# Which blocks issue their row transfers at once in a fused attention and mixture-of-experts kernel

## The chip, the core and the metric

The kernel runs on one core of one Trainium2 chip. TensorE (PE in the profile) multiplies matrices, VectorE (DVE) and ScalarE (ACT) do elementwise work, GpSimd (POOL) issues the indirect transfers, and SyncE (SP) issues the plain ones. Each engine works through its own list of instructions in a fixed order and waits on semaphores where another engine or a transfer has to be done first. The metric is device microseconds from start to end of the program, as a median over runs.

## The reference

The input x has 4 images of 256 channels and 64 x 64 pixels, in float32. Layer 0 adds an attention over each pixel's 3 x 3 neighbours. Layer 1 adds a windowed average over 64 tokens, and then a mixture of 8 experts of which each token uses its best two. Only that last part bears on the change:

```python
logits = tokens.astype(jnp.float32) @ router_w.astype(jnp.float32).T
probs = jax.nn.softmax(logits, axis=-1)
rw, re = jax.lax.top_k(probs, TOP_K)
...
for e in range(E):
    h = jax.nn.gelu(tokens @ w1[e] + b1[e], approximate=False)
    y = h @ w2[e] + b2[e]
    out = out + combine[:, e:e + 1] * y
```

## The kernel before

The 16384 tokens are cut into 32 blocks of 512 (`NB` is 32). For each block the main loop interleaves four generators: `produce` (normalise, project), `attend` (neighbour attention), `tail` (windowed average, router, store of the block's own part of the output, L685) and `ranks`, two blocks behind `attend`, which works out the row of each token in a table by experts.

**The row transfers.** `rows_in` is a table in HBM with a region for each expert. A token goes there twice, once for each of its two experts. `give(t, c)` in `ranks` (L782) is one indirect transfer of 128 token rows from SBUF to `rows_in`; a block has eight of them (4 values of t, 2 of c). They are issued by POOL (L783 in the profile). This text calls them row transfers.

**Groups and slots.** Blocks are grouped: 13 groups of two and then 6 groups of one (`GROUPS`, L85). An expert's work comes in slots of 256 rows, and there are 135 slots, numbered 0 to 134. Group 0 has 1 slot, groups 1 to 12 have 8 each, groups 13 to 17 (blocks 26 to 30) have 4 each, and the last group (block 31) has 18. So slots 101, 105, 109, 113 and 117 are the first of blocks 27 to 31.

**What a slot does** (`experts`, L889): `fetch` (L906) reads its 256 rows from `rows_in` into a tile `sx`, by SP (L912). It waits for all row transfers of the groups up to its own. `pixels` transposes them on PE (L936), `hidden` is the first product and the gelu (L948, L954), `output` the second product (L967), with bias and weight on DVE (L971, L972). `add` (L977) then adds the 256 result rows to the output in HBM by two indirect transfers that accumulate, issued by POOL (L985). This text calls them the adds, a and b of a slot. Both wait until the adds of the slot before have landed (`behind`), since two slots can hold the same token. The order of a slot's steps on PE is L936 of slot m+2, half of L967 of slot m, L948 of slot m+1, the other half of L967. The tile `sx` has 9 buffers (`rowp`, L113), so `fetch` of slot m waits for the adds of slot m-9.

**Who issues the row transfers when.** Blocks below `first_of[2]`, which is 4, issue them on the spot, in `ranks`. Those are passed through `paced` (L509), which makes them wait for the latest gelu (L954) or copy of the attention weights (L565) on ACT. Blocks from 4 on put theirs into the list `waiting`. `give_rows(2)` (L883) takes two from that list behind each slot's two adds, and `in_turn` (L871) keeps the order of adds and row transfers on POOL. `fetch` calls `give_rows(0, k)`, which issues all that is left of the groups up to its own.

Of the kernel before, what the change touches and what calls it, by code (L numbers as in the profile page):

```python
# [62 lines left out]
def hybrid_block_kernel(ctx: ExitStack, tc: tile.TileContext, ins: dict, out: bass.AP):  # L63
# [8 lines left out]
    NB = B * NBI  # L72
# [14 lines left out]
    first_of = [sum(GROUPS[:k]) for k in range(len(GROUPS))]  # L87
# [421 lines left out]
    def paced(inst):  # L509


        if latest:
            tc.add_manual_dep(
                inst.ins, latest[-1].name,
                mybir.DependencyInfo(mybir.DependencyClass.Sync, mybir.DependencyReason.DATA),
                reason="pace of the indirect transfers",
            )
        return inst
# [218 lines left out]
    def ranks(g):  # L737
        if not 0 <= g < NB:
            return
        k, j = where[g]  # L740
# [30 lines left out]
        def dispatch(inst):  # L771

            for i in range(k + 1):
                tc.declare_no_dep(
                    inst, group=f"dispatch_{i}", reason="no two tokens have one row"
                )
            tc.declare_no_dep(inst, group="fetch", reason="fetched rows are not written again")
            tc.add_to_no_dep_group(f"dispatch_{k}", inst)
            dispatched[k].append(inst)
            return inst  # L780

        def give(t, c):  # L782
            return nc.gpsimd.indirect_dma_start(  # L783
                out=rows_in[:, :],
                out_offset=bass.IndirectOffsetOnAxis(ap=rows[:, c, t : t + 1], axis=0),
                in_=tok[:, t, :], in_offset=None,
            )


        for t in range(NT):  # L790
            for c in range(2):
                if g < first_of[2]:
                    dispatch(paced(give(t, c)).ins)
                else:
                    waiting.append((k, lambda t=t, c=c: in_turn(
                        dispatch(give(t, c).ins), adds[-1:], given_rows
                    )))
            yield
# [72 lines left out]
    def in_turn(inst, others, own):  # L871

        for d in others:
            tc.add_manual_dep(
                inst, d.name,
                mybir.DependencyInfo(
                    mybir.DependencyClass.NoSync, mybir.DependencyReason.SCHED_ONLY
                ),
                reason="order of the indirect transfers",
            )  # L880
        own.append(inst)

    def give_rows(n, k=None):  # L883

        while waiting and (n > 0 or k is not None and waiting[0][0] <= k):
            waiting.pop(0)[1]()
            n -= 1
# [162 lines left out]
    for g in range(NB + 2):  # L1050
        load_xs(g + AHEAD + 2)
        channel_stats(g + AHEAD)
        gens = [attend(g), ranks(g - 2), tail(g - 1), produce(g + 1)]
        if g == 1:
            load_experts()
        n = 0
        while gens:
            for gen in list(gens):
                if next(gen, gens) is gens:
                    gens.remove(gen)  # L1060
                    continue
                n += 1
                follow(g + min(n / STEPS.get(g, 26), 0.999))
# [51 lines left out]
```

## Time and profile before

| | us |
|---|---|
| median of 3 runs (lowest to highest) | 1396.13 (1393.88 to 1398.09) |
| the profiled execution | 1398.9 |
| its span, first to last instruction | 1397.2 |
| PE busy | 1262.4 (90%) |
| DVE busy | 988.1 (71%) |
| ACT busy | 803.6 (58%) |
| POOL busy | 743.0 (53%) |

The profile is of one execution. Its span is 1.7 us shorter than that execution's time, and that time is 2.8 us above the median of the runs. The mean granted TensorE clock is 0.964 of full speed. An engine's busy time is an average over stages; which engine or transfer sets the pace has to be read stage by stage. In a row of a timeline, the numbers are start and duration in us, and the bracket gives the engine's idle time before the instruction and what is taken to have ended it. In a row of windows, busy times stand in the order PE, PE weight load, DVE, ACT, POOL, each with its count of instructions, then the granted clock, the busy share of the DMA engines and GB/s.

### The profile page before, as it was taken

The numbers are of one execution on the slowest core, as the hardware profiler recorded it, in microseconds if no ns is written. First come the engines' busy times: TensorE is split into PE (matmuls) and PEld (weight loads), VectorE is DVE, ScalarE is ACT, GpSimd is POOL, SyncE is SP. The second block draws the span as 40 slices with busy tenths as digits, with TensorE's granted clock in tenths as the row PEclk, the third lists the DMA queues.
The fourth block names the chain that finished last, engine by engine and source line by source line (L and its number), as shares of the span: only waits on it lengthen the run. The fifth ranks groups of instructions, "written<-read, shape, count | busy, mean of one in ns | idle before, by whom it ended". The sixth has DMA issues, their size and how long they took to land. (4 is left out here: it accounts for less than half of the span.)

```text
span 1397.2 us, 23159 instructions
## 1 busy us (share of the span) xinstructions
PE 1262.4 (90%) x6224; PEld 1049.8 (75%) x6224; DVE 988.1 (71%) x4649; ACT 803.6 (58%) x1605; POOL 743.0 (53%) x615
## 2 busy tenths in 40 slices
PE   5898999899999999999999999999999999859740
PEld 4677777688888878888888888888878887648530
DVE  4499988587887877787878778787867788613220
ACT  1434457666666665777776666666767665324310
POOL 2023414555665655655666556565655666654444
PEclk8999999899999999999999999999999999989975
DMA  9624444566656565666665563656565446665543
GB/s 326 245 91 131 138 160 111 148 147 142 165 111 174 125 151 128 156 151 158 155 143 129 125 159 79 159 120 147 108 168 119 90 92 151 152 143 82 81 54 38
DMA packets 147792, 190.42 MB, mean 136 GB/s; under 512 B 13776, under 2 KB 121936, under 8 KB 147536
## 3 DMA queue, kind: packets, MB, share of 16 engines
q0 software_dynamic: 51168, 71.07, 29.0%
q1 hardware_dynamic: 94000, 116.42, 26.9%
q10 hardware_dynamic: 2496, 1.45, 0.4%
q8 instruction: 52, 0.85, 0.3%
q14 instruction: 76, 0.62, 0.2%
HBM read 98.31 MB, written 90.59 MB: 135 GB/s over the span
## 5 line engine op out<-in xcount | busy, mean ns | idle before, releaser
L985 POOL DMA_INDIRECT out<-sx x270 | 431.1, 1597 | 443.8 <-DVE sx L972 126.8
L783 POOL DMA_INDIRECT rows_in<-tok,rows x256 | 267.3, 1044 | 124.2 <-issue 67.3
L967 PE MATMUL psy<-w,h 128*128 x1080 | 285.5, 387 | 10.0 <-DVE sx L971 7.2
L948 PE MATMUL psh<-xc,w1s 128*128 128x256 f32 x1080 | 260.5, 383 | 3.8 <-issue 2.8
L967 PEld LDWEIGHTS psy<-w,h 128*128 128x128 f32 x1080 | 201.7, 192 | 59.5 <-DVE sx L971 30.3
L971 DVE TENSOR_TENSOR sx<-psy,b2b 128x256 f32<-128x256 f32 x270 | 113.2, 419 | 158.2 <-PE psy L967 127.5
L948 PEld LDWEIGHTS psh<-xc,w1s 128*128 128x128 f32 x1080 | 200.9, 192 | 30.3 <-issue 4.0
L954 ACT ACTIVATE h<-psh,w1s 128x256 f32<-128x256 f32 x270 | 116.9, 478 | 104.9 <-PE psh L948 101.6
L940 ACT COPY xc<-ptx 128x512 f32<-128x512 f32 x135 | 79.6, 590 | 151.7 <-PE ptx L936 106.8
L455 PE MATMUL psv<-vo,x 128*128 128x257 f32 x528 | 131.8, 394 | 16.4 <-DVE x L437 8.7
L455 PEld LDWEIGHTS psv<-vo,x 128*128 128x128 f32 x528 | 100.9, 197 | 33.3 <-issue 7.4
L481 PE MATMUL psq<-x,qk 128*128 128x512 f32 x256 | 123.6, 592 | 0.0
L535 PE MATMUL pss<-x,q 128*128 128x256 f32 x512 | 123.2, 384 | 0.1
L572 PE MATMUL psc<-v,pT 128*128 128x256 f32 x512 | 121.8, 380 | 0.1
L572 PEld LDWEIGHTS psc<-v,pT 128*128 128x128 f32 x512 | 97.3, 190 | 26.9 <-issue 11.5
L936 PE MATMUL ptx<-ident,sx 128*128 128x128 f32 x540 | 84.2, 279 | 36.8 <-DMA sx<-rows_in 36.2
L936 PEld LDWEIGHTS ptx<-ident,sx 128*128 128x128 f32 x540 | 67.1, 146 | 57.3 <-issue 39.0
L535 PEld LDWEIGHTS pss<-x,q 128*128 128x128 f32 x512 | 95.8, 192 | 13.6 <-ACT xc L603 0.9
L972 DVE TENSOR_SCALAR sx<-sx 128x256 f32<-128x256 f32 x270 | 99.0, 367 | 4.3 <-issue 0.2
L954 ACT ACT_TABLE_LOAD x78 | 100.1, 1283 | 1.3
L552 ACT ACTIVATE pe<-logits,stop 128x259 f32<-128x259 f32 x128 | 64.3, 503 | 53.8 <-DVE stop L548 53.4
L576 DVE SCALAR_TENSOR_TENSOR xT<-psc,den,xT 128x256 f32<-128x256 f32 x128 | 55.7, 476 | 55.9 <-PE psc L572 49.3
(187 smaller groups left out, 2195.6 us busy)
## 6 DMA issues: line engine op xcount, KB each, us to landing
sx<-rows_in SPq DMA_DIRECT2D x135, 272.0 KB
xs<-in_x SPq DMA_DIRECT2D x32, 512.0 KB
xT<-in_xT SPq DMA_DIRECT2D x32, 512.0 KB
out<-xT SPq DMA_DIRECT2D x32, 512.0 KB
x<-in_x SPq DMA_DIRECT2D x24, 640.0 KB
x<-in_x SPq DMA_DIRECT2D x8, 576.0 KB
out<-sx POOLq DMA_INDIRECT x270
rows_in<-tok,rows POOLq DMA_INDIRECT x256
```

What stands on the lines that cost most here:

```text
L455: nc.tensor.matmul(ps, t[:, ci, j * P : (j + 1) * P], vo[:, ci, :], start=(ci == 0), stop=(ci == NC - 1),)
L481: nc.tensor.matmul(ps, qk[:, ci, co * P : (co + 1) * P], t[:, ci, W : W + TB], start=(ci == 0), stop=(ci == NC - 1),)
L535: nc.tensor.matmul(ps, q[:, ci, t * P : (t + 1) * P], t_[:, ci, t * P : t * P + NK], start=(ci == 0), stop=(ci == NC - 1),)
L572: nc.tensor.matmul(ps[:, u, :], pT[:, u, j, :], vals[j], start=(j == 0), stop=(j == 1))
L783: return nc.gpsimd.indirect_dma_start(out=rows_in[:, :], out_offset=bass.IndirectOffsetOnAxis(ap=rows[:, c, t : t + 1], axis=0), in_=tok[: ...
L936: nc.tensor.transpose(pt[:, c, t * P : (t + 1) * P], xs[:, t, c * P : (c + 1) * P], ident)
L948: nc.tensor.matmul(ps[:, f, :], w1s[:, o : o + P], xc[:, ci, :], start=(ci == 0), stop=(ci == NC - 1),)
L954: inst = nc.scalar.activation(h[:, f, :], ps[:, f, :], AF.Gelu, bias=w1s[:, F1 + f : F1 + f + 1])
L967: nc.tensor.matmul(ps[:, t, :], h[:, f, t * P : (t + 1) * P], w2[:, e, f, :], start=(f == 0), stop=(f == NC - 1),)
L971: nc.vector.tensor_add(ys[:, t, :], ps[:, t, :], b2b[:, e, :])
L972: nc.vector.tensor_scalar_mul(ys[:, t, :], ys[:, t, :], xs[:, t, bass.ds(e + C, 1)])
L985: inst = nc.gpsimd.indirect_dma_start(out=out, out_offset=bass.IndirectOffsetOnAxis(ap=xs[:, t, C + E : C + E + 1].bitcast(U32), axis=0), ...
```

## The change

Blocks 4 and 5, and blocks 30 and 31, now issue their row transfers in `ranks` as blocks 0 to 3 do. Before them, `give_rows(0, k)` empties the list of everything that belongs to their own group or an earlier one. Blocks 6 to 29 stay as they were.

```diff
         for t in range(NT):
             for c in range(2):
-                if g < first_of[2]:
+                if not first_of[3] <= g < NB - 2:
+                    give_rows(0, k)
                     dispatch(paced(give(t, c)).ins)
                 else:
                     waiting.append((k, lambda t=t, c=c: in_turn(
```

`first_of[3]` is 6 and `NB - 2` is 30. Lines behind this place are two higher in the new file: L985 becomes L987, L912 becomes L914.

## The prediction

> **What bounds the kernel now.** I read the table of busy times first, then windows by stage, then POOL's timeline of the last 220 us, and beside it the timelines of PE and DVE for the same slots, the chain of waits last. The windows show two regimes.
>
> ```profile
> 300.00:340.00 40.00, 39.97 (x207) 33.73 (x206) 34.04 (x164) 29.34 (x57) 25.80 (x22) 1.00 0.58 136
> ...
> 1080.00:1120.00 40.00, 40.00 (x203) 34.02 (x202) 31.62 (x161) 27.00 (x55) 25.43 (x19) 1.00 0.51 101
> ...
> 1160.00:1200.00 40.00, 38.28 (x198) 32.26 (x197) 34.20 (x184) 19.75 (x38) 27.89 (x22) 1.00 0.54 113
> 1200.00:1240.00 40.00, 26.21 (x120) 21.31 (x118) 15.15 (x65) 14.07 (x29) 27.80 (x23) 0.93 0.70 171
> 1240.00:1280.00 40.00, 33.06 (x150) 27.45 (x151) 11.27 (x29) 14.20 (x29) 19.15 (x13) 0.86 0.57 105
> ```
>
> Up to about 1170 us PE is full and sets the pace. After that it has holes, and the two largest are waits for a fetch behind the row transfers of blocks 30 and 31:
>
> ```profile
> 1214.44 1.09 PE L936 MATMUL ptx<-ident,sx 128*128 128x128 f32 x4 [5.21 <-DMA sx<-rows_in]
> ...
> 1246.38 1.08 PE L936 MATMUL ptx<-ident,sx 128*128 128x128 f32 x4 [13.82 <-DMA sx<-rows_in]
> ```
>
> They look like 19 us to be had. POOL says otherwise. Counting pairs of adds back from the last (1386.67, slot 134), 1181.72 is slot 104 and 1249.06 slot 113:
>
> ```profile
> 1181.72 1.60 POOL L985 DMA_INDIRECT out<-sx  x1 [2.29 <-DVE pj L626]
> 1183.62 1.58 POOL L985 DMA_INDIRECT out<-sx  x1 [0.30 <-DVE step L837]
> 1185.51 1.00 POOL L783 DMA_INDIRECT rows_in<-tok,rows  x1 [0.30 <-DVE first_row L860]
> 1186.81 0.98 POOL L783 DMA_INDIRECT rows_in<-tok,rows  x1 [0.30 <-issue]
> 1190.29 1.60 POOL L985 DMA_INDIRECT out<-sx  x1 [2.51 <-DVE tst_f L498]
> ...
> 1242.84 1.59 POOL L985 DMA_INDIRECT out<-sx  x1 [0.30 <-issue]
> 1249.06 1.57 POOL L985 DMA_INDIRECT out<-sx  x1 [4.64 <-issue]
> ...
> 1282.06 1.54 POOL L985 DMA_INDIRECT out<-sx  x1 [3.08 <-DMA out<-sx]
> 1283.90 1.54 POOL L985 DMA_INDIRECT out<-sx  x1 [0.30 <-issue]
> 1288.38 1.54 POOL L985 DMA_INDIRECT out<-sx  x1 [2.93 <-DVE sx L972]
> ```
>
> And two rows of DVE's timeline:
>
> ```profile
> 1228.82 0.35 DVE L972 TENSOR_SCALAR sx<-sx 128x256 f32<-128x256 f32 x1
> ...
> 1230.47 0.35 DVE L972 TENSOR_SCALAR sx<-sx 128x256 f32<-128x256 f32 x1
> ```
>
> They are slot 113's result, counted back the same way: ready at 1230.82, added at 1249.06. It was not the result that the add waited for, nor was it for any slot from 103 on; the engine that a bracket names had long been done. What it waits for is the landing of the slot before. The chain of waits has that as one piece:
>
> ```profile
> 1277.44 3.78 DMA out<-sx
> ```
>
> So a slot of the add chain takes 1.54 + 0.30 (add a), then 4.6 from issue of add b to issue of the next a, 6.45 in all. From slot 113 to the last, 21 intervals take 137.61, or 6.55 each. The last L972 ends at 1347.09 and the last add starts at 1388.51. From slot 103 (1173.37) the end is the start of the add chain plus its links. The PE holes lie under it.
>
> **The change part by part.** The instructions of PE, DVE and ACT stand in the same order in both built programs. POOL's list changes in two places, and three SP transfers move.
>
> *Blocks 4 and 5, on POOL.* Block 4's eight row transfers now stand ahead of slot 0's adds. Their rows are ready at 191.97 (L768). The pace waits are for the copy L565 that ends at 192.35, a gelu at 198.20 and a copy at 199.25. At 0.98 + 0.30 each the eight end near 205.9, and POOL is idle before from 179.6 to 207.21, so they cost 0; without that gap they would be 10.2. The four row transfers of block 5 between slot 2's adds a and b wait for a copy at 234.2, so add b moves from 235.20 to about 237.1, and four more follow. Queued behind are add 3 and the small L339 that `tail` needs: about 0.6 later than at 244.56. Its reader L620 runs at 254.21, so that is 0 too; 9 us of slack would have to go first. The first slot of blocks 4 and 5 can be fetched 17 us earlier, but PE takes it up only at 285.88, with the data landed near 267: no gain. On SP a load L130 and a store L685 move behind the fetch that needs slot 3's landing, near 252 against 251.05 and 265.97. PE is full after 280: 0.
>
> *Blocks 30 and 31, on POOL.* Before, their 16 transfers go two by two into the wait for a landing. That wait is 3.1 us, two of them take 2.6, so they are nearly free: 6.49, 6.51 and 6.55 for slots 105, 106 and 107. After, the built order is four behind slot 104's adds, four between a and b of slot 106, four behind slot 108, two behind 109, two behind 110. Their pace waits are for the gelus of slots 106 to 112, the last of which ends at 1219.86 even before, ahead of the transfer that waits for it, so they hold nothing up. Nine slots, 104 to 112, then take:
>
> - four behind a pair: 1.60 + 0.30 + 1.57 + 0.30 + 4 x 1.28 = 8.89, twice: 17.8
> - four between the adds: 1.60 + 0.30 + 5.12 + 4.6 = 11.6
> - two behind a pair: 6.5, twice: 13.0
> - none (105, 107, 111, 112): 6.45 each, 25.8
>
> Sum 68.2. Measured before, 1181.72 to 1249.06: 67.3. But that holds 8.7 of late landings (9 x 6.45 = 58.05, and 0.07 for each of eight slots with two transfers): slots 104, 108, 109, 110 and 112 take 8.57, 8.99, 8.07, 7.48 and 8.13, each while a burst is on the queues (fetches at 1181.11, 1211.04 and 1242.80, the eight blank rows from 1216.72). These bursts move, they don't go. The first now falls under a gap that POOL fills itself; block 30's fetches go off at about 1205.7 instead of 1211, onto slot 106; a store L685 on SP moves behind two more fetches and with the blank rows lies mostly under slot 108; block 31's fetches go off near 1240. No row shows this mixture. None exposed gives +0.9 in all, all of it exposed +9.6; I take 4.0 (1.7 as slot 112 for the last burst, 1.8 on slots 106 and 107, 0.5 on 109), by those rows. So the adds of slot 113 start 4.9 later.
>
> *What it buys.* Block 30 is in 5 us earlier, block 31 only about 2, since its last transfer still goes at 1237 against 1239.45. PE loses most of the 5.21 and 2 of the 13.82. Both lie under the chain: 0. If the cover were gone, it would be 7.
>
> Sum: +4.9 on the profiled execution's 1398.9, 1403.8; on the median of 1396.13, which is 2.8 lower, 1401.0.
>
> **A rule against the trace.** POOL's row is 1044 ns for a row transfer, and in the tail 0.98 with 0.30 of gap. The Trainium skill ("DMA: Bandwidth & Descriptors", section "Anatomy of one DMA — SWDGE (gpsimd) path") lists about 50 ns of dispatch and calls descriptor generation small: "You can emit a lot of descriptors before the incremental cost shows up". By that a batch of four is nearly free, every slot keeps 6.45, and nine take 58.05 + 4.0 = 62.1, 5.2 less than before: 1390.9. By the trace they take 72.2. I go by the trace, which has 526 such instructions of 1.0 to 1.6 us.
>
> **The rivals.**
>
> *The bursts stay hidden (+0.9 to +2.5, about 1398).* For: two of the gaps become POOL's own. Against: slot 106's landing is open.
>
> *The early batch was the cause of a stall (on the other side of the line).* Between 253 and 266 PE makes almost no headway: DVE idles 8.2 until 266.04, and PE is busy 4.25 of the 10 us from 260. Granted clock is 1.00 until 261, so the clock follows the stall. POOL runs from 248.91 to 265.16 without a pause, ten row transfers and two adds, and the change dissolves exactly that batch. If the batch is the cause, 8 us return where PE is the bound and carry through to slot 103: 1396.13 - 8 + 4.9 = 1393.0. It decides if the recovered time exceeds the tail's slip. Against: the eights at 94.92, 117.12, 143.50 and 166.95 did PE no such harm, and nothing names a link.
>
> *PE's tail holes count after all.* If add 113 came when its data came, 7 us would return: 1389. Slot 113's 18 us of slack speaks against.
>
> *Nothing moves in effect*: 1396.
>
> **How the numbers follow.** Likeliest: tail slip, 0.55, with 3 to 8: 1399 to 1404. Hidden bursts 0.20; stall gone 0.17; PE holes 0.04; nothing 0.04. About 0.3%, 4.2 us, is what a measurement can tell from no change: 1391.9 to 1400.3. Slower: three quarters of the first case, 0.42. Faster: half of the stall case, the PE holes, and 0.06 for the spread of runs (2 us to either side): 0.18. The same: 0.40. The range 1391 to 1405 leaves out part of the faster cases and slips above 9.
>
> **What would show it.** Right: on POOL, slot 106's adds about 7 apart and slots 104 and 108 near 8.9; adds of slot 113 3 to 8 later against the adds of slot 104, the links after it still 6.45, PE's 5 us hole gone without effect. Wrong: row transfers that take well under 1 us in a batch; a shorter 104 to 113; a PE that is busy from 253 to 266 and a slot 103 that starts some 8 earlier; or adds that start within 0.4 of their slot's L972.

## The result, and the profile after

The changed kernel takes 1390.8 us (median of ten runs, 1387.14 to 1393.86) against 1395.63 for the kernel before (ten runs, 1392.59 to 1399.9): ratio 0.9961, 95% interval 0.9943 to 0.9978, or 0.4% faster. The forecast was 1401.0, in a range from 1391 to 1405, most likely slower. The profiled execution of the changed kernel has a span of 1390.9 at a granted clock of 0.973; before it was 1397.2 at 0.964. Lines behind L790 stand two further down in the changed kernel: the adds are L987, `ptx` is L938.

What was not expected stands early. Windows of the kernel before (columns: window and length, then busy time and instructions of PE, PEld, DVE, ACT and POOL, granted clock, DMA share, GB/s):

```profile
240.00:260.00 20.00, 18.82 (x106) 16.60 (x105) 14.87 (x85) 11.24 (x22) 13.46 (x13) 1.00 0.50 140
260.00:280.00 20.00, 14.25 (x52) 10.79 (x52) 8.38 (x36) 11.63 (x22) 8.13 (x7) 0.74 0.68 158
```

and the same windows after, with two of the tail:

```profile
240.00:260.00 20.00, 20.00 (x113) 17.91 (x112) 17.53 (x101) 12.14 (x26) 11.39 (x10) 1.00 0.73 195
260.00:280.00 20.00, 20.00 (x92) 16.01 (x91) 13.04 (x44) 13.71 (x26) 10.08 (x8) 1.00 0.53 110
...
1200.00:1240.00 40.00, 23.51 (x101) 19.22 (x101) 8.23 (x21) 10.39 (x22) 25.20 (x19) 0.79 0.75 172
1240.00:1280.00 40.00, 35.49 (x172) 29.54 (x173) 13.77 (x35) 16.22 (x33) 18.63 (x12) 1.00 0.52 83
```

PE is busy 40 of 40 us between 240 and 280, where it was busy 33.07. The waits of the kernel before from 250 to 272 us show what stood there (engine and line, what it waited for, us in total, times, longest):

```profile
DVE so_far L759 <- remote: 8.2, 1, 8.2
ACT v L459 <- remote: 5.8, 2, 3.3
PEld psv L455 <- remote: 5.1, 1, 5.1
```

"remote" is a wait whose release the profile can put down to no instruction. DVE and ACT wait for results of PE (`psk`, `psv`) whose matmuls have long ended by PE's own rows; the third row is PE's own next weight load, held behind them. After the change there is no such row. The time is won there and kept: the last copy L681 ahead of that stretch comes 0.8 us later than before (256.1 against 255.3), the first of the next block 9.4 earlier (290.4 against 299.8), and add a of slot 104 comes 10.9 earlier (1170.84 against 1181.72).

The tail went as forecast, with a loss. POOL's timeline after (start, length, what; in the bracket the idle time before it and its releaser):

```profile
1170.84 1.61 POOL L987 DMA_INDIRECT out<-sx  x1 [2.31 <-DVE pj L626]
1172.75 1.59 POOL L987 DMA_INDIRECT out<-sx  x1 [0.30 <-DVE step L839]
1174.65 1.09 POOL L783 DMA_INDIRECT rows_in<-tok,rows  x1 [0.30 <-DMA sx<-rows_in]
...
1179.87 1.61 POOL L987 DMA_INDIRECT out<-sx  x1 [0.30 <-DVE tst_f L498]
...
1186.47 1.57 POOL L987 DMA_INDIRECT out<-sx  x1 [3.11 <-DVE nt_f L353]
1188.35 0.99 POOL L783 DMA_INDIRECT rows_in<-tok,rows  x1 [0.30 <-issue]
...
1193.45 1.61 POOL L987 DMA_INDIRECT out<-sx  x1 [0.30 <-issue]
1198.20 1.56 POOL L987 DMA_INDIRECT out<-sx  x1 [3.14 <-DVE first_row L862]
...
1204.72 1.55 POOL L987 DMA_INDIRECT out<-sx  x1 [3.09 <-DVE sx L974]
...
1213.54 1.61 POOL L987 DMA_INDIRECT out<-sx  x1 [0.30 <-issue]
...
1241.53 1.56 POOL L987 DMA_INDIRECT out<-sx  x1 [3.01 <-DVE sx L973]
```

Slot 104, with four row transfers behind its pair, takes 1170.84 to 1179.87, or 9.03; slot 106, with four between a and b, 11.73; slot 108 8.82. From slot 104 to slot 113 it is 70.69 instead of 67.34: 3.35 lost. Of PE's two holes the first is gone and the second is longer, since, counted from slot 104, PE comes to it some 5 us earlier and the data only 3:

```profile
1232.35 1.09 PE L938 MATMUL ptx<-ident,sx 128*128 128x128 f32 x4 [16.17 <-DMA sx<-rows_in]
```

So the two profiles read as follows: about 11 us won at 256 to 290 us, 3 to 5 lost in the tail. Whether the change wins the eleven, or the profile of before had met an accident, only runs can tell.

### The profile page after: what moved, and what is told of

Same layout as the page of the kernel before. It is cut to its first block, busy times and chain, and to the rows that moved or that the text cites. A ratio compares the mean times of both kernels' runs of the same rounds, so it can differ in the third digit from the quotient of the medians.

```text
span 1390.9 us, 23174 instructions
## 1 busy us (share of the span) xinstructions
PE 1259.6 (91%) x6224; PEld 1049.5 (75%) x6224; DVE 988.8 (71%) x4649; ACT 803.3 (58%) x1605; POOL 739.3 (53%) x615
## 5 line engine op out<-in xcount | busy, mean ns | idle before, releaser
L987 POOL DMA_INDIRECT out<-sx x270 | 430.8, 1596 | 419.7 <-DVE sx L974 88.1
L783 POOL DMA_INDIRECT rows_in<-tok,rows x256 | 264.0, 1031 | 144.6 <-issue 65.8
L455 PE MATMUL psv<-vo,x 128*128 128x257 f32 x528 | 129.7, 389 | 12.3 <-DVE x L437 8.7
L938 PE MATMUL ptx<-ident,sx 128*128 128x128 f32 x540 | 84.1, 278 | 43.7 <-DMA sx<-rows_in 43.7
L455 PEld LDWEIGHTS psv<-vo,x 128*128 128x128 f32 x528 | 99.9, 195 | 27.9 <-issue 7.4
L938 PEld LDWEIGHTS ptx<-ident,sx 128*128 128x128 f32 x540 | 66.8, 146 | 64.8 <-issue 47.6
```

Of the source, the lines that this page charges most:

```text
L455: nc.tensor.matmul(ps, t[:, ci, j * P : (j + 1) * P], vo[:, ci, :], start=(ci == 0), stop=(ci == NC - 1),)
L783: return nc.gpsimd.indirect_dma_start(out=rows_in[:, :], out_offset=bass.IndirectOffsetOnAxis(ap=rows[:, c, t : t + 1], axis=0), in_=tok[: ...
L938: nc.tensor.transpose(pt[:, c, t * P : (t + 1) * P], xs[:, t, c * P : (c + 1) * P], ident)
L987: inst = nc.gpsimd.indirect_dma_start(out=out, out_offset=bass.IndirectOffsetOnAxis(ap=xs[:, t, C + E : C + E + 1].bitcast(U32), axis=0), ...
```

## The experiments

The kernels were run in six series. In each, all kernels ran one after another on one chip, and the kernel before was timed beside them; the quoted expectations call a series a call. All ratios are to the kernel before of the same series, with 95% intervals. One table first, since the kernel before turned out to have two levels:

| series | before, us | stall in it | changed | early half alone | late half alone | four behind slots 0 to 3 |
|---|---|---|---|---|---|---|
| first comparison | 1395.63 | profiled: yes | 0.9961 | | | |
| A | 1379.92 | profiled: no | | 1.0002 (0.9990 to 1.0015) | 1.0040 (1.0024 to 1.0055) | 0.9990 (0.9979 to 1.0001) |
| B | 1396.14 | profiled: yes | 0.9964 (0.9951 to 0.9977) | | | |
| C | 1381.08 | not profiled | 1.0036 (1.0020 to 1.0052) | 1.0003 (0.9993 to 1.0012) | | 1.0003 (0.9990 to 1.0015) |
| D | 1381.65 | not profiled | | 1.0000 (0.9987 to 1.0014) | | 0.9998 (0.9986 to 1.0010) |
| E | 1396.31 | not profiled | 0.9952 (0.9936 to 0.9969) | 0.9930 (0.9905 to 0.9956) | | 0.9925 (0.9901 to 0.9950) |
| F | 1395.49 | not profiled; a variant of it: yes | 0.9955 (0.9940 to 0.9971) | | | |

### Series A: the two halves

Early half alone:

```diff
-                if g < first_of[2]:
+                if g < first_of[3]:
+                    give_rows(0, k)
                     dispatch(paced(give(t, c)).ins)
```

> Only the early half of the change: blocks 4 and 5 give out their row transfers at once, blocks 30 and 31 stay two by two behind adds. Theory A (the stall of PE between 253 and 266 us in the kernel before goes away and is carried through to the tail, while the tail's change costs 3 to 5): 10 to 11 us faster than before, median near 1385.5, and no PE gap between 250 and 270 us; it would then beat both kernels. Theory B (the early half is worth nothing, the 4.8 come from the tail, as a hole of PE that counts): within 2 us of before, 1394 to 1398. Theory C (the stall of before is an accident of the one profiled execution): within 2 us of before too, but the profile without a stall.

Measured: 1378.63 against 1379.92, ratio 1.0002 by the comparison (0.9990 to 1.0015). By itself this speaks against a gain, and it fell in a series in which the kernel before was 16 us faster than in the first comparison.

Late half alone:

```diff
-                if g < first_of[2]:
+                if g < first_of[2] or g >= NB - 2:
+                    give_rows(0, k)
                     dispatch(paced(give(t, c)).ins)
```

> Only the late half: blocks 30 and 31 give out their row transfers at once, blocks 4 and 5 stay as before. Theory A: 3.4 to 5 us slower than before, near 1400, with the stall between 253 and 266 us still there, slots 104 and 108 taking 8.9, slot 106 11.7. Theory B: 5 us faster, near 1391. Theory C: slower by 3.4 to 5 and no stall.

Measured: 1384.87, ratio 1.0040, or 4.95 us slower. Slot 104 takes 8.90, slot 106 12.33, slot 108 8.81; slots 104 to 113 take 71.64, against 66.31 in the profile of the kernel before of this series. The tail's price is the forecast's +4.9, and closing PE's first hole brings no time: theory B falls.

The kernel before, unchanged:

> The kernel before, unchanged, profiled once more. Theory A: the stall stands at the same place, PE busy under 16 of the 20 us between 260 and 280, DVE idle about 8 us before the add of so_far at 266, and the first row of POOL's tail chain (add a of slot 104) again near 1181. Theory C: PE busy 19 to 20 of 20 in that stretch, and slot 104's add near 1171.

Its windows, PE first as above:

```profile
240.00:260.00 20.00, 20.00 (x113) 17.96 (x112) 17.75 (x101) 12.12 (x26) 13.20 (x12) 1.00 0.50 139
260.00:280.00 20.00, 20.00 (x92) 16.05 (x91) 12.87 (x44) 13.73 (x26) 11.61 (x9) 1.00 0.71 186
```

There is no stall, with the same ten row transfers in a row on POOL (249.66 to 262.25) and the same load of `x` (251.80). The ten are thus not enough for a stall. Here the profile fits theory C.

Four behind each of the slots 0 to 3:

```diff
-            give_rows(2)
+            give_rows(4 if m < 4 else 2)
```

> The kernel before with four instead of two row transfers behind the adds of each of slots 0 to 3, and two behind all others; blocks 4 and 5 are so given out before the fetch that otherwise flushes ten in a row, and each stays behind adds and without pace waits. Theory A in its form A1 (the unbroken ten are the cause): the stall between 253 and 266 goes, 8 to 10 us faster, near 1386. Form A2 (what matters is that the row transfers come before slot 0's adds, or the pace waits): no faster than 2 us. Theory C: no difference beyond 2 us.

Measured: 1379.03, ratio 0.9990 (0.9979 to 1.0001): no difference, as it must be where there is no stall to take away.

### Series B: the change again

> The changed kernel, unchanged, on whatever chip this falls to. If the two halves add up as on the chip of the first four runs (early half 0, late half 5.3 slower), the whole change costs 4 to 6 us: ratio about 1.0035. If the first comparison (ratio 0.9961) tells what the change does, it is 4 to 5 us faster here too. If the stall of 10 us belongs to a chip or to a load of the kernel before and not to its order of work, the sign goes with the profile of before: a stall in it and the changed kernel is faster by about 5, none and it is slower by about 5.

> The kernel before, unchanged, profiled a third time, on the chip of the run above. With the stall between 253 and 266 us (PE busy under 16 of 20 us in 260 to 280) slot 8's adds start near 302; without it PE is busy 20 of 20 and slot 8 starts near 297.

Measured: changed 1390.3, before 1396.14, ratio 0.9964. The kernel before has the stall again, at the same place:

```profile
240.00:260.00 20.00, 17.84 (x101) 15.76 (x101) 13.55 (x80) 11.23 (x22) 13.84 (x13) 1.00 0.45 132
260.00:280.00 20.00, 15.10 (x54) 10.97 (x54) 9.63 (x38) 12.39 (x23) 8.20 (x7) 0.75 0.65 162
```

Theory C in its plain form, an accident of one execution, falls: two executions of the kernel before show the stall at the same instructions, and with it goes a level of 1396. What remains is that something is constant over a series and decides.

### Series C: the change without the stall

> Only the early half (blocks 4 and 5 at once), a second time. In the first call the kernel before ran without the stall (1379.9), and the early half was worth nothing (1.0002); in the second call it ran with it (1396.1), and the whole change was worth 0.9964. Theory D (a setting of the call, the same for all its kernels, decides whether the kernel before stalls; the early half takes the stall away where it stands, and has nothing to take where it does not): with before near 1396 this is 9 to 11 us faster, ratio 0.992 to 0.9935; with before near 1380 it is within 1.5 us, ratio 1.000. Theory E (the early half is worth nothing, the two calls differ by something else): within 2 us in both.

> Four row transfers behind the adds of slots 0 to 3 (no ten in a row), a second time. With before near 1396: if the unbroken ten beside the load of x are what PE stalls on, 9 to 11 us faster (ratio 0.992 to 0.9935), PE busy 20 of 20 between 260 and 280; if it is that the row transfers come behind adds at all, or without pace waits, the stall stays: within 2 us of before, PE busy near 15 in that stretch. With before near 1380: within 1.5 us.

> The changed kernel, a third time. Theory D: with before near 1396, 5 us faster (ratio 0.9964); with before near 1380, 4 to 6 us slower (ratio 1.003 to 1.0045), since the late half was 5 slower there and the early half nothing.

Measured: early half 1381.49 (1.0003), four behind 1380.64 (1.0003), changed 1386.57 (1.0036, 5.5 slower), with before at 1381.08. Where the kernel before does not stall, the change loses what the forecast's sum said. None of the three profiles has a stall.

Sixteen in a row, later (the early half, and blocks 6 and 7 are kept back until the fetch that needs them):

```diff
-            give_rows(2)
+            give_rows(0 if waiting and waiting[0][0] == 3 else 2)
```

> The early half, and in it the row transfers of blocks 6 and 7 are kept back until the fetch that needs them, so that sixteen stand in a row on POOL (some 21 us) behind slot 7's adds, with PE full beside them. If such a row is what PE stalls on, and with before near 1396: a stall of PE there, about 10 us or more, some 40 to 60 us later than in the kernel before, and the total 8 or more above the early half alone. If the stall needs its own place (the slots, the load of x, the block beside it): no stall, and the total within 3 us of the early half alone, or slower only by fetches that come late, which the waits of ptx would show.

Measured: 1388.38, ratio 1.0046 (1.0027 to 1.0064), 6.9 above the early half alone. Its waits from 318 to 345 us begin with

```profile
DVE tok L729 <- DMA rows_in<-tok,rows: 7.2, 1, 7.2
```

This is another stall than the one looked for: DVE may not write the next `tok` before the row transfers that read the old one have landed, and PE stands behind DVE. Since the series is at the level without the stall, the run leaves open what sixteen would do to PE where there is one; what it does show is that row transfers that are kept back hold their tile.

### Series D: a third time

> Only the early half, a third time, sought for a call in which the kernel before runs near 1396 with the stall. Theory D (the early half takes the stall away where it stands): in such a call 9 to 11 us faster, ratio 0.992 to 0.9935, PE busy 20 of 20 us between 260 and 280; with before near 1380 again 1.000. Theory E (the early half does nothing and the change of sign has another cause): 1.000 in both.

> Four row transfers behind each of the slots 0 to 3, a third time. With before near 1396: 9 to 11 us faster if the unbroken ten are what the stall needs (PE busy 20 of 20 us between 260 and 280), within 2 us with a stall if it needs only row transfers there behind adds. With before near 1380: 1.000.

Measured: 1381.77 and 1381.76 against 1381.65, ratios 1.0000 and 0.9998. Again a series at the lower level, and inconclusive on the stall.

### Series E: the halves where the kernel before is at 1396

> The changed kernel, a fourth time. With before near 1396: ratio 0.996 to 0.997; with before near 1381: ratio 1.0035. No stall between 253 and 266 us in either.

> Only the early half, beside the changed kernel. With before near 1396 (theory D): ratio 0.992 to 0.9935, 4 to 5 us below the changed kernel. Theory E: within 2 us of before. With before near 1381: 1.000, and 5 us below the changed kernel all the same.

> Four row transfers behind each of slots 0 to 3. With before near 1396: ratio 0.992 to 0.9935 if the stall needs the unbroken ten, 1.000 with a stall in the profile if it needs only row transfers there behind adds. With before near 1381: 1.000.

Measured, with before at 1396.31: changed 1389.45 (0.9952), early half alone 1386.4 (0.9930), four behind 1387.68 (0.9925 by the comparison). In the profile of the early half alone PE is full:

```profile
240.00:260.00 20.00, 20.00 (x113) 17.91 (x112) 17.47 (x101) 12.22 (x26) 11.27 (x9) 1.00 0.76 198
260.00:280.00 20.00, 20.00 (x92) 16.01 (x91) 13.24 (x44) 13.70 (x26) 10.29 (x8) 1.00 0.50 107
```

and in that of four behind it is 20.00 and 20.00 too. So theory E falls, and theory D holds as far as the level tells of the stall, since the kernel before was not profiled in this series: the early half is worth 9.9 us here, and the late half costs 3.05 (1389.45 - 1386.4). That four behind does the same shows that neither the pace waits nor the place ahead of slot 0's adds is needed. What both versions have in common is that no ten stand in a row there, and that the fetches of slots 9 to 11 go off earlier (at 253.74 with four behind in series A, 244.90 with the early half, 263.05 before). Both versions beat the kernel before in this series, and their medians lie 3.05 and 1.77 below the changed kernel; at the lower level they equal the kernel before.

### Series F: what the stall needs

> The changed kernel once more, ahead of the two below. If the stall of the kernel before stands in this call, before is near 1396 and this near 1390; if not, 1381 and 1386.

Measured: 1389.0, ratio 0.9955, before at 1395.49: a series at the upper level.

The load of `x` sent behind the fetches of slots 9 to 11, the ten left as they are:

```diff
-        load_x(g + XBUFS)
+        if g + XBUFS != 11:
+            load_x(g + XBUFS)
...
+            if m == 11:
+                load_x(11, [inst])
             return xs
```

(`load_x` hands its second argument to `in_turn`, so that the load is issued behind that fetch.)

> The kernel before with its ten row transfers in a row, and the load of x that goes off at 251 us sent behind the fetches of slots 9 to 11 instead (near 265). With before near 1396: if the stall needs this load beside the ten, 8 to 10 us faster and PE busy 20 of 20 us between 260 and 280; if the ten alone do it, within 2 us of before and a stall in the profile. With before near 1381: within 2 us.

Measured: 1395.1, ratio 0.9995 (0.9983 to 1.0008). The load now goes off at 267.91, and the stall stands:

```profile
260.00:280.00 20.00, 12.77 (x48) 9.46 (x47) 7.62 (x33) 10.50 (x20) 8.56 (x7) 0.83 0.70 197
...
DVE so_far L762 <- remote: 9.1, 1, 9.1
```

The load is not needed for it.

Three behind each of the slots 0 to 3, which leaves seven in a row:

```diff
-            give_rows(2)
+            give_rows(3 if m < 4 else 2)
```

> Three row transfers behind the adds of slots 0 to 3, so that seven stand in a row behind slot 3 instead of ten (9 us of POOL instead of 13), the load of x and the fetches in the same order as before. With before near 1396: if the stall grows with the row, some 3 to 7 us faster than before; if it needs a row that reaches past some point (the fetch of slot 9 later than about 260), 9 faster and no stall; if any row there does it, within 2 us of before. With before near 1381: within 2 us.

Measured: 1391.28, ratio 0.9966 (0.9955 to 0.9978), 4.2 faster. The stall is there, and about half as long:

```profile
260.00:280.00 20.00, 17.13 (x72) 12.40 (x71) 10.79 (x40) 13.74 (x28) 10.02 (x7) 1.00 0.73 184
...
DVE so_far L759 <- remote: 4.9, 1, 4.9
```

Ten in a row make DVE wait 8.2 to 9.1 us (three profiles) and seven 4.9; with four (series E) there is no such wait behind slot 3. There is a second regularity. POOL's last instruction without a pause, and the instruction of DVE that ends the wait, first in the kernel before, then with the load moved, then with seven in a row:

```profile
263.59 1.57 POOL L985 DMA_INDIRECT out<-sx  x1 [0.30 <-issue]
266.04 0.16 DVE L759 TENSOR_TENSOR so_far<-so_far,psk 128x8 f32<-128x8 f32 x1 [8.22 <-remote]
```

```profile
265.17 1.57 POOL L990 DMA_INDIRECT out<-sx  x1 [0.30 <-issue]
267.53 0.16 DVE L762 TENSOR_TENSOR so_far<-so_far,psk 128x8 f32<-128x8 f32 x1 [9.06 <-remote]
```

```profile
262.19 1.58 POOL L985 DMA_INDIRECT out<-sx  x1 [0.30 <-issue]
264.16 0.16 DVE L759 TENSOR_TENSOR so_far<-so_far,psk 128x8 f32<-128x8 f32 x1 [4.86 <-remote]
```

POOL's unbroken stretch ends at 265.16, 266.74 and 263.77; the wait ends 0.9, 0.8 and 0.4 us later (and 1.1 in the profile of series B, 263.95 and 265.03). So the stall lasts until about when POOL comes to rest. SP's fetch of slot 9, which waits for the row's last transfer to land, goes off at 263.05, 264.63 and 261.81 in these three, 3.0, 2.9 and 2.4 us ahead of the wait's end; whether POOL's issuing or the transfers' landing is what holds PE's results, these ends do not tell apart.

## Why the prediction was wrong, point by point

*The step that failed* is the price of the early part: "PE is full after 280: 0". Its covers were rightly read for the new order, but what the old order cost was put at nothing as well, although the same profile showed DVE idle for 8.2 us beside the very row that the change dissolves. At the upper level that row costs 9.9 us instead of 0 (series E: 1396.31 before, 1386.4 with the early half); at the lower level 0 was right (1.0002, 1.0003, 1.0000). The text had the stall as a rival (0.17, 1393.0) and put against it that earlier rows of eight did PE no harm and that no link was named. Neither was a reason to price it at 0. Nor did PE stand still from 253 on, as the rival has it: its rows run at full rate to 258.4, and what stands is the word that they are done (last section). The rival's sum, -8 + 4.9, came within 2.2 us of the result with both its terms off (9.9 and 3.05 in series E), so that its nearness is in part luck.

*What the chance should have been.* One profile could not tell an accident from a cause. But the three runs shown (1393.88 to 1398.09) stood near the profiled one, 1398.9, which had the stall in it, so an accident of that one execution was the less likely reading. A forecast that starts from that execution's time carries the stall along, and has to say what becomes of it.

*The tail* was right in form and a little too dear on one term. Slot 104 was forecast at 8.89 and took 9.03, slot 106 11.6 and 11.73, slot 108 8.89 and 8.82. The contention term, put at 4.0, was 2.5 (70.69 less the 68.2 of the working): the last burst made one slot longer as foreseen, though it was slot 111 (8.02) and not 112, but slots 106 and 107, where 1.8 was expected, paid 0.2. In the runs the late half costs 4.95 (A, alone), 5.1 (C, by difference) and 3.05 (E, by difference), against +4.9.

*The rule weighed against the trace.* The trace was right: a row transfer in the tail's bursts costs POOL 0.96 to 1.09 and 0.30 of gap, and a slot with four of them grows from 6.5 to 9. The rule's 1390.9 is near the result, but by another way; its shorter 104 to 113 did not come, that stretch grew by 3.35.

*PE's holes* lie under the add chain, as said: the first went, the second grew from 13.82 to 16.17 where it was to shrink by 2, and neither shows in the total.

*The clock.* It was read as following the stall, and that holds: with seven in a row PE loses 2.87 of 20 us and the granted clock stays 1.00, with ten it is 0.74 to 0.83. The Trainium skill ("TensorE: Matmul & The Clock Gate", "Part 1: The HAM clock gate (the "warmup" mystery)") has the gate close after an idle window of about 3.4 us. This trace fits that only roughly: in the kernel before, the half clock begins at 261.4, some 3 us after PE's rows begin to thin out (258.5), and PE's rows still fill 1.1 of these 3 us.

*The same forecast* would have been close in series C, where the change took 5.5 us more: 1.0036 against a forecast of 1.0035. Its sum was that of a kernel that does not stall, put on the time of one that does.

## What to carry to other kernels

A stall that stands in the profile of before is part of the time of before: when a change dissolves what runs beside it, give its removal a price, even where no releaser is named, or find out by a second profile whether it recurs. Indirect transfers that are queued behind other work and flushed together by whoever needs them form long rows on POOL; let them out a few at a time, early, where they have cover (four behind each early slot did as well as giving them out at once: some 9 us in series E, nothing at the lower level), and leave the tail's two by two where the add chain on POOL sets the pace. Where an engine waits for results whose instructions have long ended, look for when the signal of their end came, and not only for when they ran. Compare two versions only within one series, for a level of 15 us came and went here between series, and it decided the sign.

## What the hardware showed that was not expected

In some series a row of indirect transfers on POOL holds back PE's results: ten, with two adds behind them (16.3 us of POOL), make DVE wait 8.2 to 9.1 us and cost 10 in the total; seven (12.5 us) 4.9, and by estimate some 6 (10 less the 4.2 won). The hold ends as POOL comes to rest. In the kernel before, PE's rows for `psv` and ACT's copies of it stand so:

```profile
253.48 1.90 PE L455 MATMUL psv<-vo,x 128*128 128x257 f32 x8
...
261.70 0.38 ACT L459 COPY v<-psv 128x257 f32<-128x257 f32 x1 [3.32 <-remote]
264.52 0.37 ACT L459 COPY v<-psv 128x257 f32<-128x257 f32 x1 [2.44 <-remote]
```

What holds them in between, the trace behind the profile narrows down. Beside the rows it keeps the time of each rise of the semaphore that PE raises when a group of matmuls is done, and on which the other engines wait. The end of a group's last row, and the rise that belongs to it in order, in us:

| group of matmuls | before: row ends | before: semaphore rises | series A, no stall: row ends | series A, no stall: semaphore rises |
|---|---|---|---|---|
| `psy` L967 | 253.64 | 256.70 | 254.39 | 254.40 |
| `psv` L455, first | 254.51 | 261.68 | 255.25 | 255.27 |
| `psv` L455, second | 255.38 | 264.50 | 256.12 | 256.14 |
| `ptp` L563 | 255.81 | 265.96 | 256.56 | 256.57 |
| `psk` L753 | 256.18 | 266.02 | 256.93 | 256.94 |
| `ptx` L936 | 256.65 | 266.08 | 257.40 | 257.41 |
| `psp` L614 | 257.58 | 266.17 | 258.32 | 258.34 |
| `psh` L948 | 262.98 | 266.26 | 260.05 | 260.07 |

The last five rises come within 0.30 us, although `psp` and `psh` alone are 16 matmuls, which take 2.8 us in series A. So the multiplying was done before, and what came late were PE's signals. The copies of ACT and the add of DVE at 266.04 start within 0.03 us of theirs.

This sorts the two levels. In all ten traces from series at the lower level every signal of PE comes within 0.016 us of its row's end. In all ten at the upper level some are late: by up to 10.7 us in the stall behind ten row transfers and 6.3 behind seven, and by 2.3 to 2.6 at most in the traces without a stall, four behind slots 0 to 3 among them. Even the rows of eight ahead of 200 us hold them there, by 1.2 us at most. Signals over 1 us late come at twelve places between 320 and 1150 us in each of these ten traces, once in a group of two blocks for the most part, beside four row transfers in a row on POOL. The signals of DVE and ACT are never over 0.06 us late there. What POOL's rows and PE's signals share, no run shows.

Nor is it settled what makes a series one or the other. The chips recorded were numbers 7, 5 and 12 at the lower level, and 7, 7 and 14 at the upper: the number does not sort them. In the series at the upper level the changed kernel stands first on record, in the others the early half alone does; that order was not tried as a cause. Something else differs: the traces at the upper level hold 15164 to 15491 rises of semaphores, those at the lower 20248 to 20266, for nearly the same instructions. Records are thus missing at the upper level, and whether the recording itself holds PE's signals there, or suffers from the same cause, was not tried either. If it does, the stall and the gain of the early half belong to how the kernel was timed.

Beside the stall, the upper level costs some 2 to 9 us more in kernels without one (early half alone 1386.4 against 1378.6 to 1381.8, four behind 1387.7 against 1379.0 to 1381.8, changed 1389.0 to 1390.8 against 1386.6). For the early half alone, PE in the trace of series E falls 5.2 us behind that of series C between 300 and 1100 us. Most of that comes in steps behind a late signal, of 0.2 to 0.5 us each and of about 2 near 1010 us; a step of 1.6 near 815 us follows none, so that a part stays open.
